# Attention scores as seven block products for each pair of key chunks, half-features and query blocks

## The chip, the cores and the metric

One core of a Trainium2 chip runs the whole program. The time is the device time of one launch in microseconds, as a median over launches. The profile is one execution of its own, with its own time. The engines of the core are TensorE (PE, with its weight loads PEld), VectorE (DVE), ScalarE (ACT), GpSimd (POOL) and SyncE (SP), which issues nearly all DMAs.

## The reference

A block of a transformer: a layer norm, then attention with one head of 512 features, and beside it a mixture of 64 low-rank experts of which each token takes 16; both are added to the input.

```python
xn = _layernorm(x)                                   # x: (2, 2048, 2048)
# attention
qkv = einsum('bsc,cf->bsf', xn, Wqkv) + bqkv         # (2, 2048, 3 * 512)
q, k, v = qkv.reshape(2, 2048, 3, 512) ...
attn = softmax(einsum('bqd,bkd->bqk', q, k) / sqrt(512))
att = einsum('bqd,dc->bqc', einsum('bqk,bkd->bqd', attn, v), Wo) + bo
# experts
scores = einsum('bsr,er->bse', einsum('bsd,rd->bsr', xn, Wq_w), keys)
gate = softmax over the 16 greatest of the 64 scores, 0 elsewhere
z = einsum('bsd,nd->bsn', xn, A_w)                   # 64 experts x 8
ffn = einsum('bsn,on->bso', gate * z, B_w) * 2
return x + att + ffn
```

All is float32.

## The kernel before

**Arithmetic.** Each float32 operand of a large product is split into a high part (a cast to the rounded type `fp32r`, `split_hi`, on ACT, L123) and a low part (the rest, `split_lo`, on DVE, L126). A product of two operands is three matmuls into one PSUM bank, low x high, high x low and high x high (`PASSES`, L60; `product`, L128). A matmul is 128x128 weights against 512 moving columns.

**Stages.** The 4096 tokens are 8 blocks of 512 (`NB`), four to a sequence (`BPB`). First come the projections: q, k, v, the router and the experts' first product; for the last three pairs of blocks these run as seven phases P1, P2, P6, P5, P3, P7, P4 of Strassen's scheme (`phase`, L755), each with steps on DVE and ACT dealt out beside its matmuls by `beside` (L663). Then comes the attention stage (L1226 to L1281). Last comes the output projection, `multiply` at L1164 and its neighbours, also by Strassen's scheme, for both the attention and the experts at once. P1 and P2 of that scheme share a PSUM bank: P2 is added onto P1.

**What the projections leave for the attention.** `feature_out` (L499) takes one 128-feature tile of q or k for a block out of PSUM, adds the bias, splits it into high and low parts and stores both ([128, 2, 512], 512 KB) to `q_d` or `k_d` in DRAM. `values_out` (L274) does the same for v.

**The attention stage.** A step `s` is one query block of 512 (`blk`) and one chunk of 128 keys (`k`, 16 a sequence). `score` (L935) multiplies the chunk's four feature tiles (`kt`, weights) with the block's (`qt`, moving): 4 x 3 matmuls into one bank, the scores transposed, keys on partitions. ACT copies the bank to SBUF (L950), DVE keeps a running maximum (L954, L956). After a block's 16 chunks `maxes` (L958) reduces the maximum over partitions, and `spread` (L982) lays it on all partitions with a matmul. `soft` (L990) subtracts it, takes the exponential on ACT, splits the result into `ph` and adds the sum `L`. `weigh` (L1005) loads the chunk's values `vt` and multiplies: for each of the four feature tiles three matmuls onto that tile's bank, over 16 chunks. At the end of a block the sum goes through two matmuls and a reciprocal (L1024 to L1027), the four banks are scaled (L1032), get their bias (L1033) and go to DRAM.

In program order each step scores chunk `s`, softens chunk `s - 18` and weighs chunk `s - 21` (`LAG`, L32); so scores and weighted values alternate on PE, with 21 steps of scores alone at the front and 21 of weighted values alone at the end. Four of the seven banks of `acc` (L100) hold a block's values, three serve the scores.

Beside it, `combos` (L1051) makes the sums of output weights that the last stage needs: loads, four additions on POOL, two stores, for eight pieces. In the last 12 steps and after, the first splits of the output weights (`moving`, L1063) and of its moving operands (`ahead`, L1211) are made.

**Order.** The scheduler of the language orders each engine's queue by program order as priority, among what its own model finds ready; `with behind(...)` keeps the instructions in its block behind a named one on the same engine. Tiles named by a `Ring` share slots in turn, and a tile waits until the readers of the one before it in the slot are done. Each engine runs its queue in order.

Of the kernel before, what the change touches and what calls it, by code (L numbers as in the profile page):

```python
# [16 lines left out]
P = 128  # L17
C = 2048
NCH = C // P
D = 512  # L20
# [11 lines left out]
LAG = 21  # L32
# [31 lines left out]
def attn_ffn_kernel(ctx: ExitStack, tc, x, xT, wq, wv, wob, bqk, bv, bo, keysT, out):  # L64
# [6 lines left out]
    KC = 2 * ND  # L71
# [66 lines left out]
    q_d = [scratch(f"q_d{i}_", ND) for i in range(NB)]  # L138
    k_d = [scratch(f"k_d{i}_", ND) for i in range(NB)]
# [359 lines left out]
    def feature_out(i, f, ps, gx, u=None):  # L499
        kind, n = divmod(f, ND)  # L500
        if kind < 2:
            ev = r_ev([P, 2, T], FR, "ev")
            b = bqk_sb[:, f : f + 1]
            if u is None:
                nc.scalar.activation(ev[:, 0, :], ps, AF.Identity, bias=b)
                nc.vector.scalar_tensor_tensor(
                    ev[:, 1, :], ps, b, raw(ev[:, 0, :]), ALU.add, ALU.subtract
                )
            else:
                v = raw(ev[:, 1, :])  # L510
                nc.vector.scalar_tensor_tensor(v, ps, b, u, ALU.add, ALU.add)
                split_hi(ev[:, 0, :], v)
                split_lo(ev[:, 1, :], v, ev[:, 0, :])
            store((k_d if kind else q_d)[i][n], raw(ev))
# [148 lines left out]
    def beside(j, ph):  # L663
# [18 lines left out]
        if ph == "P6":  # L682
            return [], mixed(
                sum_steps(j, nc.vector, b10, b10, b00, ALU.subtract),
                sum_steps(j, nc.vector, b00, b11, b00, ALU.subtract), split_steps(j, "P5", *b00),
                s0[:-2] if more else [],
            )
        if ph == "P5":
            steps = mixed(split_steps(j, "P3", *b11), s1[:-2] if more else [])
            return [], s0[-2:-1] + steps[:6] + s0[-1:] + steps[6:] if more else steps  # L690
        if ph == "P3":
            n = x_steps(j + 1, *b00) if more else ([], [])
            steps = mixed(split_steps(j, "P7", *b01), n[1][:2])
            return n[0], s1[-2:-1] + steps[:3] + s1[-1:] + steps[3:] if more else steps
        if ph == "P7":
            n = x_steps(j + 1, *b10) if more else ([], [])
            return n[0], mixed(split_steps(j, "P4", *b10), n[1][:2])
# [4 lines left out]
        return [], []  # L702
# [106 lines left out]
    NSTEP = NB * NK  # L809
    kt, qt, S, pt_, M, L, av, rl_ = {}, {}, {}, {}, {}, {}, {}, {}  # L810

    def load_k(b, kb):
        for dc in range(ND):
            t = r_kt([P, 2, T], FR, "kt")
            nc.sync.dma_start(raw(t), k_d[b * BPB + kb][dc])
            kt[b, kb, dc] = t

    def load_q(blk):
        for dc in range(ND):
            t = r_qt([P, 2, T], FR, "qt")  # L820
            nc.sync.dma_start(raw(t), q_d[blk][dc])
            qt[blk, dc] = t
# [68 lines left out]
    for j in PAIRS:  # L891
        for ph in PHASES:
            if j == PAIRS[-1] and ph == "P7":
                sA, sB, sC, sD = GROUPS
                r_kt = big(*sC, *sB, *T_SLOTS[:8])
                r_qt = big(*sD, 6, 7, 8, 9)
            if j == PAIRS[-1] and ph == "P4":
                load_q(0)
                load_k(0, 0)
                load_k(0, 1)  # L900
# [3 lines left out]
    s_slots = [*sA, *T_SLOTS[8:], 27, 28]  # L904
    r_sp = big(*s_slots)
# [3 lines left out]
    r_mbc = half(4)  # L909
    r_L = half(5, 6)  # L910
# [3 lines left out]
    r_tw = Ring(sb, "B25", "B26", "B29", "G8", "G9")  # L914
    r_ph = wide(0, 1, 2, 3)
    r_vt = wide(4, 5, 6, 7)
# [18 lines left out]
    def score(s):  # L935
        blk, k = divmod(s, NK)
        b = blk // BPB
        ps = acc()
        sl = slice((k % NT) * P, (k % NT + 1) * P)
        for dc in range(ND):  # L940
            product(
                ps, lambda a: kt[b, k // NT, dc][:, a, sl], lambda c: qt[blk, dc][:, c, :],
                dc == 0, dc == ND - 1,
            )
# [412 lines left out]
```

## Time and profile before

| | us |
|---|---|
| median of 3 runs | 2640.55 |
| lowest and highest | 2639.7, 2644.24 |
| the profiled execution's own time | 2641.34 |
| its span, first to last instruction | 2639.6 |
| first score matmul to last weighted value | 1320 to 2026 |

In the profile a group of instructions is a line of the code with its engine, operation, output and inputs; "busy" is the time in which at least one of them ran, "mean" the duration of one, and instructions of one engine overlap in part. "Idle before" is what the engine stood still ahead of them, with what released it. A row of stages gives busy time of each engine, the granted TensorE clock, the mean busy share of the 16 DMA engines and what they moved.

### The profile page before, as it was taken

The numbers are of one execution on the slowest core, as the hardware profiler recorded it, in microseconds if no ns is written. First come the engines' busy times: TensorE is split into PE (matmuls) and PEld (weight loads), VectorE is DVE, ScalarE is ACT, GpSimd is POOL, SyncE is SP. The second block draws the span as 40 slices with busy tenths as digits, with TensorE's granted clock in tenths as the row PEclk, the third lists the DMA queues.
The fourth block names the chain that finished last, engine by engine and source line by source line (L and its number), as shares of the span: only waits on it lengthen the run. The fifth ranks groups of instructions, "written<-read, shape, count | busy, mean of one in ns | idle before, by whom it ended". The sixth has DMA issues, their size and how long they took to land.

```text
span 2639.6 us, 33827 instructions
## 1 busy us (share of the span) xinstructions
PE 2624.7 (99%) x12881; PEld 2220.4 (84%) x12881; DVE 1822.3 (69%) x2495; ACT 863.6 (33%) x1285; POOL 571.8 (22%) x347
## 2 busy tenths in 40 slices
PE   8999999999999999999999999999999999999999
PEld 7889888888888888888888888888888888888887
DVE  7667859867878688756545675456568776797775
ACT  4333323333333333333233343334344222232221
POOL 1312420000000000000101111000012656566664
PEclk9999999999999999999999999999999999999999
DMA  6777884768556683546725476634468545565543
GB/s 234 254 260 256 310 299 166 228 222 295 162 173 221 218 291 129 176 128 222 287 97 192 143 268 227 210 112 144 130 204 267 172 162 165 177 222 172 180 158 106
DMA packets 243395, 530.42 MB, mean 201 GB/s; under 512 B 21608, under 2 KB 87200, under 8 KB 243232
## 3 DMA queue, kind: packets, MB, share of 16 engines
q1 hardware_dynamic: 230272, 498.37, 55.9%
q10 hardware_dynamic: 12960, 29.89, 3.4%
q8 instruction: 101, 1.65, 0.2%
q14 instruction: 62, 0.51, 0.1%
HBM read 393.80 MB, written 134.38 MB: 200 GB/s over the span
## 4 chain that ended last, share of the span: by engine, by line
PE 98%; DVE 1%; DMA 0%; ACT 0%; issue 0%; SPq 0%; ACTq 0%; DVEq 0%
PE acc L131 75%; PE acc L1172 23%; DMA xs<-in_x 0%; DVE st L196 0%; PE acc L366 0%; DVE xh L126 0%; PE misc L451 0%; PE misc L984 0%; DVE wh L126 0%; DMA v_d<-vs 0%; PE misc L1024 0%; PE misc L1025 0%; PE misc L481 0%; ACT xh L123 0%; ACT xs L357 0%
## 5 line engine op out<-in xcount | busy, mean ns | idle before, releaser
L131 PE MATMUL acc<-t,pw 128*128 128x512 f32 x3024 | 693.4, 390 | 0.0
L131 PEld LDWEIGHTS acc<-t,pw 128*128 128x128 f32 x3024 | 565.4, 188 | 117.4
L1172 PE MATMUL acc<-wb,s 128*128 128x512 f32 x2688 | 609.4, 389 | 0.0
L1172 PEld LDWEIGHTS acc<-wb,s 128*128 128x128 f32 x2688 | 504.5, 188 | 104.8
L131 PE MATMUL acc<-ph,vt 128*128 128x512 f32 x1536 | 367.5, 390 | 0.0
L131 PE MATMUL acc<-qt,kt 128*128 128x512 f32 x1536 | 366.0, 389 | 0.0
L131 PEld LDWEIGHTS acc<-ph,vt 128*128 128x128 f32 x1536 | 287.4, 188 | 62.1 <-DVE ot L1032 1.2
L131 PEld LDWEIGHTS acc<-qt,kt 128*128 128x128 f32 x1536 | 288.1, 188 | 60.3 <-issue 0.2
L1156 POOL TENSOR_TENSOR xo<-xo,bo_bc 128x512 f32<-128x512 f32 x128 | 217.0, 1702 | 551.0 <-DMA xo<-in_x 292.1
L123 ACT CAST pw<-pw 128x1024 fp32r<-128x1024 f32 (+1 forms) x168 | 177.7, 1058 | 373.8 <-PE acc L131 252.3
L126 DVE TENSOR_TENSOR pw<-pw 128x1024 fp32r<-128x1024 f32 (+1 forms) x168 | 217.6, 1296 | 67.3 <-ACT pw L123 67.1
L131 PE MATMUL acc<-xh,wh 128*128 128x512 f32 x1152 | 263.6, 390 | 0.0
L131 PEld LDWEIGHTS acc<-xh,wh 128*128 128x128 f32 x1152 | 215.6, 188 | 45.0
L131 PEld LDWEIGHTS acc<-pw,t 128*128 128x128 f32 x2016 | 245.8, 188 | 3.2 <-DVE yv L746 2.0
L131 PE MATMUL acc<-pw,t 128*128 128x264 f32 x2016 | 246.5, 283 | 1.8 <-DVE yv L746 1.8
L123 ACT CAST s<-xz 128x1024 fp32r<-128x1024 f32 x112 | 118.0, 1055 | 371.5 <-PE acc L1172 301.5
L126 DVE TENSOR_TENSOR s<-xz,s 128x1024 fp32r<-128x1024 f32 x112 | 173.2, 1548 | 42.0 <-ACT s L123 42.0
L126 DVE TENSOR_TENSOR ph<-sp,ph 128x512 fp32r<-128x512 f32 x128 | 93.0, 729 | 120.6 <-ACT ph L123 119.8
L956 DVE TENSOR_TENSOR M<-M,sp 128x512 f32<-128x512 f32 x112 | 79.1, 706 | 124.3 <-ACT sp L950 123.8
L521 POOL TENSOR_TENSOR zt<-zt,g 128x512 f32<-128x512 f32 x24 | 37.5, 1572 | 496.4 <-DVE zt L520 148.1
L126 DVE TENSOR_TENSOR wh<-wu,wh 128x512 fp32r<-128x512 f32 x96 | 99.3, 1055 | 58.8 <-ACT wh L123 58.8
L950 ACT COPY sp<-acc 128x512 f32<-128x512 f32 x128 | 74.9, 586 | 182.6 <-PE acc L131 182.5
(149 smaller groups left out, 2365.9 us busy)
## 6 DMA issues: line engine op xcount, KB each, us to landing
vt<-v_d SPq DMA_DIRECT2D x128, 512.0 KB, 3.5
pw<-sq_d SPq DMA_DIRECT2D x72, 512.0 KB, 3.6
xz<-oz_d SPq DMA_DIRECT2D x64, 512.0 KB, 4.9
xo<-in_x SPq DMA_DIRECT2D x128, 256.0 KB, 3.5
out_y<-xo SPq DMA_DIRECT2D x128, 256.0 KB, 2.3
pw<-in_wq SPq DMA_DIRECT2D x54, 512.0 KB, 4.0
wu<-in_wq SPq DMA_DIRECT2D x48, 512.0 KB, 5.8
xq<-in_xT SPq DMA_DIRECT2D x48, 512.0 KB, 6.8
```

Of the source, the lines that this page charges most:

```text
L123: return nc.scalar.copy(hi, src)
L126: return (eng or nc.vector).tensor_tensor(lo, src, raw(hi), ALU.subtract)
L131: last["pe"] = nc.tensor.matmul(ps, st(a_), mv(b_), start=first and n == 0, stop=end and n == 2)
L521: nc.gpsimd.tensor_tensor(zt, zt, gx[n], ALU.mult)
L950: nc.scalar.copy(st, ps)
L956: nc.vector.tensor_tensor(M[blk], M[blk], st, ALU.max)
L1156: nc.gpsimd.tensor_tensor(xs, xs, bo_bc[q // (NB // 2 * NH), c], ALU.add)
L1172: nc.tensor.matmul(ps, st[a_][:, kk, sl], mv[b_], start=not more and kk == 0 and n == 0, stop=kk == ND - 1 and n == 2, skip_group_check=more,)
```

## The change

Keys, features and queries are each cut in two: two chunks of 128 keys, two halves of 256 features, two blocks of 512 queries. The four score tiles of a chunk pair and a block pair took 4 x 12 = 48 matmuls; they become seven products of 256 features, 7 x 6 = 42 matmuls. `ORDER` names them as the other stages do.

- `feature_out` stores q and k unsplit, 256 KB a tile.
- `key_steps` loads a block's keys for one 128-feature tile of each half, makes the seven key operands with four subtractions or additions of 256 elements, splits them, and writes them to `kp_d`. The steps for key blocks 0 to 4 run beside the last pair's phases P6, P5 and P4, those for 5 to 7 inside the attention stage.
- `query_steps` makes the four sums of queries of a block pair and writes them to `qs_d`; pairs 0 and 1 beside phases P3 and P7, pairs 2 and 3 in the attention stage. `query_load` and `query_split` fetch and split an operand.
- `key_load` streams the key operands through a ring of five tiles of two operands each, for every block pair anew.
- `score(g)` makes one product and combines it; a block pair's 56 products come in a row, and weighted values of the pair before are dealt between them. So the first 65 products run without weighted values and the last pair's values without scores.
- `soft` subtracts and takes exponentials two chunks at a time; `ph` has three slots in place of four.
- `combos` adds on DVE in place of POOL and has eight DMAs of 256 KB in place of four of 512 KB.

```diff
 def feature_out(i, f, ps, gx, u=None):
-            ev = r_ev([P, 2, T], FR, "ev")
+            ev = r_ev([P, T], F32, "ev")
             if u is None:
-                nc.scalar.activation(ev[:, 0, :], ps, AF.Identity, bias=b)
-                nc.vector.scalar_tensor_tensor(
-                    ev[:, 1, :], ps, b, raw(ev[:, 0, :]), ALU.add, ALU.subtract
-                )
+                nc.scalar.activation(ev, ps, AF.Identity, bias=b)
             else:
-                v = raw(ev[:, 1, :])
-                nc.vector.scalar_tensor_tensor(v, ps, b, u, ALU.add, ALU.add)
-                split_hi(ev[:, 0, :], v)
-                split_lo(ev[:, 1, :], v, ev[:, 0, :])
-            store((k_d if kind else q_d)[i][n], raw(ev))
+                nc.vector.scalar_tensor_tensor(ev, ps, b, u, ALU.add, ALU.add)
+            store((k_d if kind else q_d)[i][n // 2][:, n % 2, :], ev)
...
+    ORDER = ("P1", "P6", "P2", "P5", "P3", "P7", "P4")
+    ks = {"R": big(25, 26), "st": big(27, 28, 29, 9)}
+    def key_steps(kb, d):
...
+        def one(step):
+            a00, a01, a10, a11 = (quad(a, h) for a in range(2) for h in range(2))
+            tt = nc.vector.tensor_tensor
+            out()
+            src = {"P1": a00, "P2": a01, "P4": a11, "P5": a11, "P7": a10, "P6": a00, "P3": a01}[step]
+            if step == "P5":
+                tt(a11, a10, a11, ALU.add)
...
+            st = ks["st"]([P, 2, 2, P], FR, "kst")
+            split_hi(st[:, :, 0, :], src)
+            split_lo(st[:, :, 1, :], src, st[:, :, 0, :])
+            v["out"] = kp_d[kb][ORDER.index(step)][:, :, :, d, :], raw(st)
...
+    def query_load(j, n):
...
+        hi, lo = (r_qt([P, 2, T], FR, "qt") for k in range(2))
+        nc.sync.dma_start(raw(lo), src)
+        qop[j, n] = hi, lo
...
+    def key_load(i):
...
+        t = r_kt([P, 2, 2, 2, P], FR, "kt")
+        for o in range(2):
+            st, n = divmod(2 * i + o, 7)
+            j, m = divmod(st, NKS)
+            kb = j // 2 * BPB + m // 2
+            last["sp"] = nc.sync.dma_start(raw(t[:, o]), kp_d[kb][n][:, m % 2])
+            kop[2 * i + o] = t[:, o]
...
+                r_qt = big(*sC, *sD, *sA, *sB)
+                r_kt = big(*T_SLOTS[:3], 25, 26)
...
-    r_ph = wide(0, 1, 2, 3)
-    r_vt = wide(4, 5, 6, 7)
+    r_ph = wide(0, 1, 2)
+    r_vt = wide(3, 4, 5, 9)
...
+    def score(g):
+        st, n = divmod(g, 7)
+        j, m = divmod(st, NKS)
+        b0, b1 = 2 * j, 2 * j + 1
+        step = ORDER[n]
+        more = step == "P2"
+        ps = bank["P1"] if more else acc()
+        bank[step] = ps
+        k, q = kop.pop(g), qop[j, n]
+        for d in range(2):
+            for i, (a, c) in enumerate(PASSES):
+                last["pe"] = nc.tensor.matmul(
+                    ps, k[:, a, d, :], q[c][:, d, :],
+                    start=not more and d == 0 and i == 0, stop=d == 1 and i == 2,
+                    skip_group_check=more,
+                )
+        tt = nc.vector.tensor_tensor
+        if step == "P1":
+            nc.scalar.copy(unit(b0, m)[:, 1, :], ps)
+        u, v = S[b0, m], S.get((b1, m))
+        if step == "P6":
+            tt(u[:, 1, :], u[:, 1, :], ps, ALU.add)
+        elif step == "P2":
+            nc.scalar.copy(u[:, 0, :], ps)
+        elif step == "P5":
+            tt(unit(b1, m)[:, 1, :], u[:, 1, :], ps, ALU.add)
+            greatest(b0, m, 0)
+        elif step == "P3":
+            tt(v[:, 0, :], v[:, 1, :], ps, ALU.add)
+            greatest(b1, m, 0)
+        elif step == "P7":
+            tt(v[:, 1, :], v[:, 1, :], ps, ALU.add)
+            tt(u[:, 1, :], u[:, 1, :], ps, ALU.add)
+            greatest(b1, m, 1)
+        elif step == "P4":
+            tt(u[:, 1, :], u[:, 1, :], ps, ALU.add)
+            greatest(b0, m, 1)
...
+        if k % 2 == 0:
+            nc.vector.tensor_tensor(
+                u, u, mbc[blk].unsqueeze(1).to_broadcast([P, 2, T]), ALU.subtract
+            )
+            nc.scalar.activation(u, u, AF.Exp, scale=SCALE)
...
+    begin = [NG1 * (j + 1) + (9 if j in (0, NPAIR - 1) else 5) for j in range(NPAIR)]
+    for i in range(4):
+        key_load(i)
...
+    for n, (kb, d) in enumerate(((5, 0), (5, 1), (6, 0), (6, 1))):
+        deal(2 + 11 * n, key_steps(kb, d))
...
+    deal(NG1 + 10, [small_ring] + key_steps(7, 0) + key_steps(7, 1))
+    deal(NG1 + 38, query_steps(2, r_tp), 2)
+    deal(2 * NG1 + 7, query_steps(3, r_tp), 2)
...
+    for j in range(1, NPAIR):
+        deal(NG1 * j - 14, [lambda j=j: query_load(j, 0), lambda j=j: query_split(j, 0)], 4)
+        for n in range(1, 7):
+            deal(NG1 * j - 7 + n, [lambda j=j, n=n: query_load(j, n), lambda j=j, n=n: query_split(j, n)], 3)
...
+    for g in range(begin[-1]):
+        if g < total:
+            score(g)
+            if g % 2:
+                key_load(g // 2 + 4)
...
+        for i in range(NPAIR - 1):
+            if begin[i] <= g < begin[i + 1]:
+                to = NW * i + NW * (g + 1 - begin[i]) // (begin[i + 1] - begin[i])
+                while done < to:
+                    weigh(done)
+                    done += 1
```

Here `NG1` is 56 (products of a block pair), `NW` 128 (weighted products of a block pair, three matmuls each), `NKS` 8 (chunk pairs) and `NPAIR` 4.

## The prediction

> **What bounds the kernel now.** I read the page from the top: first the busy shares and the chain that ended last, then the matmul groups, then the chain in order of time inside the attention stage, then the busy time of every engine by stage.
>
> ```profile
> PE 2624.7 (99%) x12881; PEld 2220.4 (84%) x12881; DVE 1822.3 (69%) x2495; ACT 863.6 (33%) x1285; POOL 571.8 (22%) x347
> ...
> PE 98%; DVE 1%; DMA 0%; ACT 0%; issue 0%; SPq 0%; ACTq 0%; DVEq 0%
> ...
> L131 PE MATMUL acc<-ph,vt 128*128 128x512 f32 x1536 | 367.5, 390 | 0.0
> L131 PE MATMUL acc<-qt,kt 128*128 128x512 f32 x1536 | 366.0, 389 | 0.0
> ```
>
> TensorE is the bound: 98% of the chain is PE. The scores are 1536 matmuls (`qt,kt`), the weighted values another 1536 (`ph,vt`); no idle time stands before either. That a busy PE really issues without gaps is seen in the chain in order of time:
>
> ```profile
> 1369.71 76.36 PE acc L131 x336
> 1446.07 0.43 PE misc L984
> 1446.50 13.80 PE acc L131 x60
> 1460.30 0.24 PE misc L1024
> 1460.54 0.23 PE misc L1025
> 1460.77 73.59 PE acc L131 x324
> ```
>
> 336 matmuls in 76.36 us and 324 in 73.59 are 227.2 ns each (the 389 of the groups is latency, not pace). So a matmul taken out is worth 0.2272 us as long as nothing else becomes late.
>
> **The gain.** Before, 8 blocks x 16 key chunks x 12 matmuls = 1536. After, 4 block pairs x 8 chunk pairs x 7 products x 6 matmuls = 1344. 192 x 0.2272 = 43.6 us, all in a stage where PE never waits. Everything else is what that gain may lose; no term below can be negative, since PE has no wait left to give up in these stages. The new stage needs 1344 + 1536 matmuls = 654 us, plus 8 x (0.43 + 0.24 + 0.23) = 7, so 661 us.
>
> **VectorE.** What it has to do follows from these rows:
>
> ```profile
> 1388.11 1.89 DVE L993 TENSOR_TENSOR sp<-sp,mbc 128x512 f32<-128x512 f32 x3
> ...
> 1391.51 2.88 PE L131 MATMUL acc<-ph,vt 128*128 128x512 f32 x12
> 1391.71 0.59 ACT L950 COPY sp<-acc 128x512 f32<-128x512 f32 x1 [0.69 <-PE acc L131]
> ```
>
> Three operations of 512 take 1.89 us where one takes 0.68, so back to back each costs 0.605. In the same way 1024 elements cost about 1.14 (1.22 alone, less 0.08) and 256 about 0.345 (0.41 to 0.43 for 248 and 264 elements alone, less 0.075). Per chunk pair and block pair the scheme needs 6 PSUM additions and 4 maxima: 10 x 0.605 = 6.05, times 32 = 191 after the saved first maxima. The exponentials need 16 subtractions of 1024, 32 low parts and 30 sums per pair: 18.2 + 19.4 + 18.2 = 55.8, times 4 = 223. Each block's end (maximum spread 3.0, reciprocal 3.35, four outputs 2.4, low part 0.6) is 9.4, times 8 = 75. New in the stage: 21 query low parts x 1.14 = 24; 6 key steps x 11 operations x 0.345 = 23; query sums 16 x 0.605 = 10; `combos`, moved from POOL, 32 x 0.605 = 19; the weight splits and sums for the output projection, there before too, 16. Total 581 of 661 us, 88%; before it was 55% to 63%. By stretch: 85 of 88.6 in the scores of the first pair alone (65 products x 1.363 before the first weighted value), 403 of 470 in the middle, 93 of 102 after the last score.
>
> ```profile
> 1099.00:1143.00 44.00, 44.00 (x241) 38.41 (x240) 29.03 (x31) 13.28 (x14) 3.53 (x2) 1.00 0.42 136
> 1143.00:1188.00 45.00, 45.00 (x251) 39.50 (x250) 21.36 (x24) 13.32 (x14) 0.00 (x0) 1.00 0.45 142
> 1228.00:1231.00 3.00, 3.00 (x15) 2.47 (x14) 2.52 (x3) 2.39 (x3) 0.00 (x0) 1.00 0.72 170
> 1320.00:1378.00 58.00, 58.00 (x257) 47.64 (x256) 24.06 (x45) 17.64 (x33) 0.00 (x0) 1.00 0.29 103
> 1730.00:1818.00 88.00, 88.00 (x388) 72.39 (x387) 48.67 (x78) 31.79 (x54) 0.00 (x0) 1.00 0.41 132
> 1969.00:2026.00 57.00, 57.00 (x250) 46.42 (x249) 51.62 (x73) 27.74 (x44) 15.56 (x5) 1.00 0.81 275
> 2026.00:2100.00 74.00, 74.00 (x328) 61.29 (x327) 53.69 (x53) 20.32 (x23) 37.47 (x23) 1.00 0.60 199
> ```
>
> Columns: stretch, length, busy PE, weight load, DVE, ACT, POOL, clock, DMA share, GB/s. The row of 1969 shows DVE 51.6 of 57 us (91%) with PE full: so 86% in the middle and 91% in the tail need not cost PE anything; 96% in the first stretch is beyond what was seen. I take **0 for the tail** (bounds 0 and 5) and **1 for the middle** (0 and 8). Moving `combos` to DVE is free: with POOL adding beside it, the subtraction L993 takes 853 ns mean against 685 without, and windows with it hold some 55 us of DVE instead of 48.7 for two `combos`, more than the 4.8 us they cost on DVE itself; they issue 8 DMAs each in place of 4, at times when SP has some 2.9 us per product. ACT keeps room: it stays near 32 us a block, of 88 before and 82 after.
>
> **DMA.** The last two columns give a full-share rate: 103/0.29 = 355 GB/s for 4 KB rows, 199/0.60 = 332 for 2 KB rows, 170/0.72 = 236 around the four `gd<-gT` writes in 512 B pieces, which is how the key operands are written. In the first score stretch must move: 65 key operands of 0.262 MB (17.0 MB, 51 us), 8 key loads (2.1 MB, 6), 28 key writes in 512 B pieces (7.3 MB, 31), 7 query operands and 3 value tiles (5.2 MB, 15). That is 103; less 6 for the eight operands fetched earlier, 97 of 88.6 us: 8.6 late. All at 355 would give 87 and no delay. With DVE operations at their full 0.68 (95.5 us) another 7 is lost. SP has 111 DMAs to issue there at 0.32 to 0.57 us, 36 to 63 of 88.6. Behind a late transfer, or a key write that waits for DVE, stand the next ones in SP's queue, key operands too, only 8 products ahead. At the stretch's end the second pair's query operands can be fetched only when the first pair's last product of the same kind is done: 7 products or 9.5 us ahead, where landing (7.4 median of `qt`), cast (1.05) and low part (1.14) take 9.6; there the delay should show first. Bounds 0 and 16; **I take 8**, the nearest rows' value. The Trainium skill ("DMA: Bandwidth & Descriptors", Specifications) puts full rate at 512 B and above; by that the 31 would be 21, this term nothing, and the time 2605; the 236 measured here differs, and I keep it.
>
> Ahead of the stage, phases P6 and P5 of the last pair get 3 and 5 key steps, each 1.6 us of loads and 7.8 of writes. P6: 0.42 x 44 + 28 = 47 of 44; P5: 0.45 x 45, less four `qt` loads that go (5.9), + 47 = 61 of 45. So 19 us of transfers spill into P3. PE is hurt only if weights come late; SP issues them between the key writes, at most four of which (4.4 us) can be under way in the four-slot ring. Weight loads land in 3.6 us, up to 10.7, with no PE wait now. **I take 3**; bounds 0 and 19. VectorE there rises to 21.4 + 19 = 40 of 45, covered as above. The plain stores of q and k save 48 low parts and half the bytes; in a stage bound by PE that is worth nothing.
>
> **Buffers.** P2 adds into P1's bank, so PE waits for ACT's copy of P1 while P6 (1.36 us) runs. The copy begins 0.20 after the next product and takes 0.59: 0.57 to spare, less when a 1.05 us cast is ahead on ACT; behind that wait stand all later matmuls. **I take 1** (0 to 5; in the middle 2.3 weighted products more lie between). At a block's end four banks wait for reciprocal and outputs, with one score fewer in between than now; the trace has 1.2 us of such waits over eight blocks, four outputs each time would be 2 x 8. **I take 3** (1 to 16). The change from the projections to the scores: key operands can be fetched during P4, since their slots are free after P7. **0** (to 7, if they stood behind the last value stores).
>
> **Sum.** -43.6 + 8 + 3 + 1 + 3 + 1 = -27.6. The profiled execution took 2641.3 us (span 2639.6); that becomes 2613.7. The median of the runs is 0.8 lower, so **2613 us**. All lower bounds together lose 1: 2598. All upper ones lose 76: 2673.
>
> The skill ("TensorE: Matmul & The Clock Gate", Part 1) says PE falls to half clock after an idle window of about 3.4 us. The clock is 1.00 in each row above, as no PE wait here is that long after the start; if the 8 us came in one piece, the recovery would add an estimated 1.7 us.
>
> **Rivals.**
> *Nothing is late.* The buffers take up all peaks, as PE without a gap at 91% DVE suggests: 2598 to 2604. Against it: the 97 of 88.6 us of DMA.
> *The transfers set the pace* wherever key operands are written: the whole 16 and 19 lost, 2626 to 2635. For it: 512 B pieces at 236 GB/s. Against: weights have slack of several us.
> *Slower: VectorE paces the scores.* Each product needs its bank freed by an addition queued in order on DVE, with four of seven banks held by the values. If additions stand behind waiting softmax work so that an operation costs on average 25% more than 0.605, the stretches need 106, 504 and 116 of 88.6, 470 and 102 us: 66 lost, **2663 us**. It decides from about 21% on (0.735 us an operation). For it: DVE idles 120 us before `ph` for ACT and 124 before `M`, a sign of its in-order waits. Against: those waits harm nobody now, at 91% in the tail too.
>
> **Chances.** 2604 to 2626, my forecast: 0.35. Nothing late: 0.25. Transfers pace: 0.12. Within 0.2% (about what a measurement of this kernel can tell from no change, 5.3 us): 0.05. Slower: 0.23, most of it between 2646 and 2670. So faster 0.72, same 0.05, slower 0.23. The range is 2598 to 2652, with some 0.15 above it and 0.03 below; faster cases alone end at 2635.
>
> **What would show it.** Score matmuls x1344 at 227 ns; DVE near 88% in the stage; PE waits, if I am right, in the first 89 us of scores and the two phases P6 and P5, with a key tile's DMA or a DVE addition as releaser; DMA share near 1 there. If the attention stage is 661 us and free of waits, the DMA term is wrong; if PE waits for DVE all through the middle, the rival on VectorE is right.

## The result and the profile after

The changed kernel took 2653.95 us (median of 6 runs, 2648.07 to 2655.96) against 2642.05 of the kernel before on the same chip (6 runs, 2639.70 to 2644.24): a ratio of 1.0042, 95% interval 1.0029 to 1.0055. It is slower by 0.4%, where 1.1% faster was forecast; the side that was given 0.23 came true, and the time lies 2 us above the stated range. The profiled execution took 2654.26 us, its span is 2652.4.

The page first: busy shares, chain, and the two matmul groups of the attention.

```profile
PE 2604.3 (98%) x12689; PEld 2197.6 (83%) x12689; DVE 1982.9 (75%) x2827; ACT 858.9 (32%) x1249; POOL 519.9 (20%) x315
...
PE 31%; DVE 1%; DMA 0%; issue 0%; ACT 0%; SPq 0%; DVEq 0%; ACTq 0%
...
L129 PE MATMUL acc<-ph,vt 128*128 128x512 f32 x1536 | 381.0, 393 | 6.1 <-DMA vt<-v_d 2.8
...
L1062 PE MATMUL acc<-qt,kt 128*128 128x512 f32 x1344 | 342.1, 397 | 16.9 <-ACT sp L1069 10.3
```

The 192 matmuls are gone. The chain's shares add up to some 32% only: followed back from the last instruction, it breaks off near 1770 us, so it can't be set beside the 98% of before and tells nothing of the stage's first part. What does tell is the idle time before both groups (16.9 and 6.1 us), where there was none. PE's waits from the phases P6 and P5 to the first score, and then in the attention stage, tell for what (us in total, times, longest):

```profile
PE acc L129 <- ACT t L121: 4.6, 1, 4.6
PE acc L129 <- DVE yv L755: 2.3, 1, 2.3
```

```profile
PE acc L1062 <- ACT sp L1069: 10.3, 3, 5.9
PE misc L1115 <- DVE mq L1105: 4.7, 4, 1.8
PE acc L1062 <- DVE qt L124: 4.4, 5, 1.3
PE acc L129 <- DMA vt<-v_d: 2.8, 1, 2.8
PE acc L129 <- DVE ph L124: 1.9, 1, 1.9
PE acc L1062 <- DMA kt<-kp_d: 1.9, 1, 1.9
```

The greatest one is ACT's copy of P1 (L1069), for which P2 waits because it adds onto the same bank. Only 1.9 us of these waits are for a key operand's transfer. All waits in the stage, smaller ones too, come to 27.5 us.

To see how much was lost where, I cut the time at four points of PE's timeline (first score, first weighted value, last score, first matmul of the output projection) and took off what the matmuls of each piece need at 0.2272 us: 398 in the scores alone (90.4 us), 2030 in the middle (461.2, with 6 for the small matmuls of the block ends 467), 451 in the tail (103.2 with its share of those). "Ahead" is how much later than before (1320.15) the scores begin. The same cut of every kernel profiled, in us lost:

| kernel | ahead | scores alone | middle | tail | sum | time of that execution |
|---|---|---|---|---|---|---|
| predicted | 3 | 8 + 1 | 3 + 1 | 0 | 16 | 2613.7 |
| changed kernel | 12.7 | 27.2 | 7.4 | 11.0 | 58 | 2654.26 |
| a_no_keys56 | 17.5 | 10.6 | 4.9 | 10.9 | 44 | 2639.74 |
| c_loads_early | 17.0 | 16.2 | 4.5 | 7.4 | 45 | 2640.95 |
| d_half_stream | 12.7 | 14.8 | 10.3 | 10.0 | 48 | 2644.47 |
| e_phases_ahead | 13.3 | 16.4 | 7.4 | 6.9 | 44 | 2639.98 |
| f_maxima_later | 15.3 | 25.7 | 6.7 | 10.3 | 58 | 2653.9 |
| g_tail_loads_ahead | 16.2 | 25.9 | 7.2 | 3.6 | 53 | 2649.62 |
| h_all_ahead | 9.3 | 15.5 | 6.7 | 3.8 | 35 | 2632.3 |
| j_keys67_later | 10.7 | 17.0 | 17.6 | 5.7 | 51 | 2647.41 |
| i_keys4_later | 14.1 | 8.5 | 13.8 | 4.5 | 41 | 2638.14 |

Sum less 43.6, less some 1 us that the stage of before loses by the same cut, is the change of the span: 58 - 45 = 13 here, and 2652.4 - 2639.6 is 12.8. Four rows (changed kernel, a, f, g) have the same code up to the first score and differ there by 12.7 to 17.5, so a difference of 5 us in that column is no finding by itself. In the first score stretch the changed kernel and g still have the same code, f all but its last ten products, and they lose 25.7 to 27.2. The rows of c_loads_early and h_all_ahead are the fastest run of each kernel, and so favourable ones.

What a wait in the first score stretch looks like, from the timeline of all engines (start, duration, engine, line, operation; in brackets the idle time before it and what ended it):

```profile
1338.22 11.70 PE L1062 MATMUL acc<-qt,kt 128*128 128x512 f32 x42 [2.47 <-ACT sp L1069]
...
1346.42 0.43 DVE L288 TENSOR_TENSOR vs<-acc,xv 128x264 f32<-128x264 f32 x1 [7.53 <-DMA v_d<-vs]
...
1351.46 1.12 SPq L834 DMA_DIRECT2D kr<-k_d  x2
...
1354.90 0.40 ACT L121 CAST kst<-kr 128x256 fp32r<-128x256 f32 x1 [6.75 <-DMA kr<-k_d]
1355.21 0.58 ACT L1069 COPY sp<-acc 128x512 f32<-128x512 f32 x1
```

ACT stands for 6.75 us before a cast of raw keys (`kr`) whose load SP issued only at 1351.46; P1's copy is the next instruction in ACT's queue and has to stand with it; PE gets going at 1355.84, after 5.92 us. Eight us earlier DVE stood for 7.53 us in the same way, before the last projection's values, whose slot was still being stored. Here neither ACT nor DVE was short of time. Each had one instruction at the head of its queue that waited for a transfer. SP was one more link between the two: it issued nothing from 1342.52 to 1348.00, as the next store of those values waited for DVE, and the load of `kr` stood behind that store. From SP's waits in the stretch:

```profile
SPq L162 <- DVE vs L124: 5.4, 1, 5.4
```

The stretch as a whole, its first 30 us, what lies between, its last 22 us, and a window of the middle stage (start and end, length, busy PE, weight load, DVE, ACT, POOL, granted clock, DMA share, GB/s):

```profile
1332.85:1450.45 117.60, 100.86 (x401) 77.97 (x399) 88.95 (x169) 33.05 (x65) 0.00 (x0) 0.93 0.92 304
1332.85:1362.85 30.00, 21.60 (x80) 16.65 (x79) 15.88 (x35) 6.87 (x17) 0.00 (x0) 0.83 0.88 273
1362.85:1428.45 65.60, 61.83 (x255) 49.49 (x254) 51.68 (x97) 16.53 (x35) 0.00 (x0) 0.95 0.96 313
1428.45:1450.45 22.00, 17.44 (x68) 11.83 (x66) 21.40 (x39) 9.65 (x13) 0.00 (x0) 1.00 0.85 321
...
1824.00:1846.00 22.00, 22.00 (x98) 18.22 (x98) 22.00 (x34) 9.28 (x12) 0.00 (x0) 1.00 0.90 309
```

By the matmuls that start in each piece, 12 us are lost in the first, 8 in the second and 7 in the third. DVE is busy for 89 us of the 117.6 (76%); at 1824 it is busy all the time and PE loses nothing, so a busy DVE alone doesn't make PE wait. But in the last 22 us it is busy for 21.4 (97%), and there PE's five waits for the low parts of the next query operands (`qt`, 4.4 us) end with DVE. The DMA share of the stretch is 92% at 304 GB/s, which is 35.8 MB.

### The profile page after: what moved, and what is told of

It reads as the page before. It is cut to its first block, busy times and chain, and to the rows that moved or that the text cites. A ratio compares the mean times of both kernels' runs of the same rounds, so it can differ in the third digit from the quotient of the medians.

```text
span 2652.4 us, 34800 instructions
## 1 busy us (share of the span) xinstructions
PE 2604.3 (98%) x12689; PEld 2197.6 (83%) x12689; DVE 1982.9 (75%) x2827; ACT 858.9 (32%) x1249; POOL 519.9 (20%) x315
## 5 line engine op out<-in xcount | busy, mean ns | idle before, releaser
L1320 POOL TENSOR_TENSOR xo<-xo,bo_bc 128x512 f32<-128x512 f32 x128 | 210.8, 1654 | 914.5 <-DMA bo_bc<-in_bo 609.6
L129 PE MATMUL acc<-ph,vt 128*128 128x512 f32 x1536 | 381.0, 393 | 6.1 <-DMA vt<-v_d 2.8
L1062 PE MATMUL acc<-qt,kt 128*128 128x512 f32 x1344 | 342.1, 397 | 16.9 <-ACT sp L1069 10.3
L1062 PEld LDWEIGHTS acc<-qt,kt 128*128 128x128 f32 x1344 | 256.1, 192 | 77.0 <-ACT sp L1069 11.8
L124 DVE TENSOR_TENSOR wh<-wu,wh 128x512 fp32r<-128x512 f32 x96 | 81.0, 860 | 99.4 <-ACT wh L121 99.4
L121 ACT CAST ph<-sp 128x512 fp32r<-128x512 f32 x128 | 78.9, 619 | 167.2 <-PE acc L129 161.1
L1325 DVE TENSOR_TENSOR xo<-xo,acc 128x512 f32<-128x512 f32 x128 | 86.9, 680 | 54.8 <-PE acc L1336 26.0
L121 ACT CAST t<-xq 128x1024 fp32r<-128x1024 f32 x84 | 88.0, 1051 | 94.3 <-DVE xq L648 41.0
```

Of the source, the lines that this page charges most:

```text
L121: return nc.scalar.copy(hi, src)
L124: return (eng or nc.vector).tensor_tensor(lo, src, raw(hi), ALU.subtract)
L129: last["pe"] = nc.tensor.matmul(ps, st(a_), mv(b_), start=first and n == 0, stop=end and n == 2)
L1062: last["pe"] = nc.tensor.matmul(ps, k[:, a, d, :], q[c][:, d, :], start=not more and d == 0 and i == 0, stop=d == 1 and i == 2, skip_group ...
L1320: nc.gpsimd.tensor_tensor(xs, xs, bo_bc[q // (NB // 2 * NH), c], ALU.add)
L1325: nc.vector.tensor_tensor(xs, xs, ps, op)
```

## The experiments

The theory after the result: ACT and DVE stand behind key steps that wait for their own transfers, and what PE needs stands behind them. The rivals: VectorE and ScalarE have too much to do; or the transfers of the stretch as a whole set its length.

**a_no_keys56: no key preparation in the first score stretch.** Key blocks 5 and 6 are not prepared; the scores of the second sequence take the operands of blocks 1 and 2 instead, so the stream is the same.

```diff
             kb = j // 2 * BPB + m // 2
+            kb = {5: 1, 6: 2}.get(kb, kb)
...
-    for n, (kb, d) in enumerate(((5, 0), (5, 1), (6, 0), (6, 1))):
-        deal(2 + 11 * n, key_steps(kb, d))
```

> The key steps of key blocks 5 and 6, dealt inside the first stretch of scores, are left out, and their operands are read from blocks 1 and 2 (so pairs 2 and 3 score other keys). The stretch took 117.6 us for 399 matmuls that need 90.6. Theory one, in-order engines stand behind key casts and low parts that wait for their own transfers: without them the stretch is 92 to 97 us, with at most the query waits at its end left (some 5 us), and the program 20 to 25 us shorter, near 2630. Theory two, the key stream that PE reads sets the pace: the stream is still there, so the stretch stays above 105 us. Theory three, VectorE is full there: it loses 15 us of its 85, and the waits for query low parts (4.4 us) shrink but the long waits for ACT's copy of P1 stay: above 105 us.

The stretch fell from 117.6 to 101.0 us, and one run took 2639.74. That is less than the other two theories gave (above 105) and more than mine did (92 to 97); the time is 10 us above mine. So 16.6 of the 27 lost there come with the four key steps, by their work, their waits or their transfers: the stretch moved 262 GB/s x 101 us = 26.5 MB. One wait of 3.4 us for P1's copy stayed at the stretch's start, where the key steps of phase P4 are still being finished.

**b_keys_pool: the arithmetic of all key steps on GpSimd**, so that ACT and DVE have nothing of it in their queues.

```diff
-            tt = nc.vector.tensor_tensor
+            tt = nc.gpsimd.tensor_tensor
...
-            split_hi(st[:, :, 0, :], src)
-            split_lo(st[:, :, 1, :], src, st[:, :, 0, :])
+            nc.gpsimd.tensor_copy(st[:, :, 0, :], src)
+            split_lo(st[:, :, 1, :], src, st[:, :, 0, :], nc.gpsimd)
```

> All arithmetic of the key steps (casts, sums, low parts, 18 operations each, all 16 steps) goes to POOL; transfers are the same. Theory one (in-order ACT and DVE stand behind key work that waits for transfers): the waits move to POOL, where nothing else is late, so the first stretch falls from 117.6 to 92 to 100 us and the phases before the scores from 12.6 us late to under 4: 2615 to 2625 in all, faster than before. Theory two (transfers set the pace): within 5 us of the changed kernel, 2649 to 2659. Theory three (VectorE is full): VectorE gains 15 us in the stretch, but POOL's reads slow it; 2640 to 2650.

Far off: 2716.6 us (2713.68 to 2724.99), ratio 1.0286 (1.0266 to 1.0306). The scores begin at 1380.95, 61 us later than before; the stretch takes 129.5. PE's waits ahead of the first score:

```profile
PE misc L454 <- ACT qT L449: 11.3, 1, 11.3
PE acc L129 <- ACT t L121: 10.0, 1, 10.0
PE acc L129 <- ACT pw L121: 9.8, 2, 8.0
PE acc L129 <- DVE pw L124: 8.9, 3, 6.7
```

On average a low part takes 856 ns on POOL against 420 on DVE, a sum 972 to 1077 against 416 to 490, and the phases now wait for operands of their own (`t`, `pw`) on ACT and DVE. Which transfers or slots pass the lateness on was not followed further; the run doesn't tell the theories apart.

**c_loads_early: the same work and transfers, but the raw keys are loaded a step ahead** (two steps' loads beside the first key operands, four slots instead of two), in the first stretch alone.

```diff
-    ks = {"R": mid(0, 1), "st": wide(0, 1, 2, 3, 4, 5)}
+    ks = {"R": mid(2, 3, 0, 1), "st": wide(0, 1, 2, 3, 4, 5)}
...
+    for n, steps in enumerate(early):
+        if n > 1:
+            deal(2 + 11 * (n - 1), steps[:1])
+        deal(3 + 11 * n, steps[1:])
```

> In the first stretch the loads of the key steps of blocks 5 and 6 are issued one step (some 15 us) earlier, into four slots in place of two; all else stays. Theory one in its narrow form (ACT waits at the head for the key load, 5.9 us once): the wait of ACT's casts for the key loads goes, the stretch falls by 8 to 14 us to 104 to 110, the program to 2640 to 2646. If it is the store slots or the transfers at large: no change beyond 3 us.

In the profiled execution, the fastest of ten, the stretch took 106.6 us, 11 less with nothing taken out of it: that much was waiting, not work. The time is 2646.68 (2640.95 to 2652.51, 10 runs), ratio 1.0017 (1.0006 to 1.0027), just above the 2640 to 2646 expected; the median is 7 us below the changed kernel's. ACT's greatest wait before a key cast changed its cause. In the changed kernel, from the first score to the first weighted value:

```profile
ACT kst L121 <- DMA kr<-k_d: 20.2, 7, 7.4
```

and here:

```profile
ACT kst L121 <- DMA kp_d<-kst: 24.3, 14, 5.3
```

The load is there in time, and the cast now waits for its output slot, which is still being stored. PE still waits 5.1 us for P1's copy behind it. The stretch, and the part between its first 30 and its last 22 us, and these last, in the columns of above:

```profile
1337.10:1443.70 106.60, 96.77 (x401) 76.00 (x399) 88.75 (x168) 32.20 (x63) 0.00 (x0) 0.97 0.99 337
1367.10:1421.70 54.60, 54.60 (x243) 45.22 (x242) 48.74 (x91) 15.21 (x31) 0.00 (x0) 1.00 1.05 366
1421.70:1443.70 22.00, 17.26 (x65) 11.13 (x63) 21.65 (x40) 9.32 (x13) 0.00 (x0) 1.00 0.88 320
```

It moves as much as before, 337 GB/s x 106.6 us = 35.9 MB, at a DMA share of 0.99. Yet the transfers are not what holds PE: in the 54.6 us between, at a share of 1.05 (a packet counts where it starts), PE never stands. What is still lost lies at the two ends: 8 us in the first 30, around one wait of 4.2 us for P1's copy, and 8 in the last 22, where DVE is busy for 21.65.

**d_half_stream: half the traffic of key operands**, all key steps in place. Only the first operand of each tile is loaded and stands for both.

```diff
-            last["sp"] = nc.sync.dma_start(raw(t[:, o]), kp_d[kb][n][:, m % 2])
-            kop[2 * i + o] = t[:, o]
+            if o == 0:
+                last["sp"] = nc.sync.dma_start(raw(t[:, o]), kp_d[kb][n][:, m % 2])
+            kop[2 * i + o] = t[:, 0]
```

> Every second key operand is not loaded; its product uses the one before it in the tile (other scores). This takes 29 of the 59 MB of the key stream away and leaves all engine work. Theory two (transfers set the pace): the first stretch falls below 98 us, the tail keeps its 114, the program 20 us shorter. Theory one (engines in order behind key casts that wait for their own loads and stores): these come sooner with less traffic, but wait still: 105 to 114 us. Theory three (VectorE): unchanged, 115 to 118.

The stretch took 105.2 us, one run 2644.47:

```profile
1332.80:1438.00 105.20, 94.99 (x399) 75.53 (x397) 86.22 (x166) 33.37 (x65) 0.00 (x0) 0.97 0.80 251
```

26.4 MB at a share of 0.80: the transfers have room, and the stretch is hardly shorter than c's, as expected if waits set it (105 to 114). PE waits 6.8 us for P1's copies, and ACT 14.6 in place of 20.2 before a cast for its load. Less traffic shortens the waits as earlier loads do, and leaves the same two ends: 9 us are lost in the first 30 and 5 in the last 22.

The second round took the four places one by one.

**e_phases_ahead: raw keys one step ahead in the phases P6, P5 and P4**, with four slots, and other slots for stores in P4.

```diff
+    KSL = [key_steps(m // 2, m % 2) for m in range(10)]
+    def key_part(a, b):
+        return [
+            st for m in range(a, b)
+            for st in (KSL[m + 1][:1] if m < 9 else []) + KSL[m][1:]
+        ]
...
-    ks = {"R": big(25, 26), "st": big(27, 28, 29, 9)}
+    ks = {"R": Ring(sb, "B25", "B26", "H6", "H7"), "st": big(27, 28, 29, 9)}
```

> Only the key steps ahead of the scores change: each step's loads are issued one step (about 9 us) earlier, into four slots in place of two, and P4's two steps store from four slots in place of two. Same instructions, same bytes. In the changed kernel the scores begin 12.6 us later than before (1332.8 against 1320.2) and lose 10.7 us more in their first 20 us. If ACT and DVE stand at the head of their queues for key loads and store slots: the scores begin at 1321 to 1326 and the first 20 us lose under 6. If it is the number of bytes in P6 and P5 or DVE's load there: they begin at 1330 to 1335 as now.

Where it was expected to help it did not: the scores begin at 1333.4, 0.6 us later than in the changed kernel. The wait for `t` fell from 4.6 to 1.0, the one for `yv` rose from 2.3 to 4.9. But the stretch behind it took 106.8 instead of 117.6: phase P4 no longer hands its unfinished key steps on to the scores. One run took 2639.98.

**f_maxima_later: the block's maxima three products later, its two spreads one and four** in program order, as their matmul waits for DVE.

```diff
-            if n == 1:
+            if n == 4:
                 maxes(2 * j - 2)
-            if n in (0, 2):
+            if n in (1, 6):
...
-                    spread(2 * j - 1 - n // 2)
+                    spread(2 * j - 1 - n // 6)
```

> The partition maxima of a pair's first block go three products later and both spreading matmuls one and four products later in program order. In the changed kernel PE waits 4.7 us in four places for the spread's operand from DVE, with some more lost to the clock. If DVE is late only at the change of pairs, these waits fall below 1.5 us, the middle from 474.4 to 468 to 471 us. If DVE is late throughout, other waits for DVE take their place and the middle stays within 2 us.

Nothing was gained: 2653.9. The waits for `mq` fell from 4.7 to 3.0 us, a new one of 2.0 for the scaled outputs `ot` came in their place, and the middle is 6.7 against 7.4. That is what was expected if DVE is late throughout the middle and not only where pairs change.

**g_tail_loads_ahead: output weights loaded one piece at a time in the tail, and split two chunks later**, instead of two pieces loaded and split at once with value tiles behind them in SP's queue.

```diff
-        if d == 0 and c in (2, 6, 10, 14):
-            for kk in range(0, ND, 2):
-                with behind("sp"):
-                    for st in moving(0, STEPS[c // 4], kk):
-                        st()
+        if d == 0 and c % 2 == 0 and 2 <= c <= 18:
+            with behind("sp"):
+                if c > 2:
+                    splits[c // 2 - 2]()
+                if c < 18:
+                    one_load, one_split = moving(0, STEPS[(c - 2) // 4], (c - 2) % 4)
+                    one_load()
+                    splits.append(one_split)
```

> After the last score the loads of the output weights go one by one, two chunks ahead of their splits, in place of two at once just before them. In the changed kernel the tail takes 114.2 us for 102.3 us of matmuls; PE waited 2.8 us for values queued on SP behind a load of output weights that waited for its slot, and 1.9 us for a low part behind splits and a reciprocal on DVE. If it is SP's queue: the tail falls to 106 to 109 us. If it is DVE's load (some 91%): it stays at 112 to 116.

The tail fell from 114.2 to 106.8 us. The waits of 2.8 us for `vt` and 1.9 for `ph` are gone from it. DVE's work there is the same, so the 11 us of the tail were mostly SP's order.

**h_all_ahead: e, f and g together, and the early loads of c** with other slots.

```diff
+    early = [key_steps(kb, d) for kb, d in ((5, 0), (5, 1), (6, 0), (6, 1))]
     for i in range(4):
         key_load(i)
+        if i < 2:
+            early[i][0]()
```

> The three edits of this call and early loads of the key steps in the first stretch together. If the lateness is that of in-order queues behind transfers, the parts add: 12.6 to about 4 ahead of the scores, 27 to about 14 in the first stretch, 9 to 5 in the middle, 12 to 6 in the tail: some 30 us off the changed kernel's 2653, so 2618 to 2630, faster than before by 0.5 to 0.9%. If the transfers or DVE as a whole were the bound, lateness only moves to the next place: 2643 to 2653.

2638.85 us (2632.3 to 2646.74, 12 runs) against 2642.77 (17 runs): ratio 0.9985 (0.9976 to 0.9995). That is faster than before by 0.15%, and less than expected (2618 to 2630). What is left at the start of the scores:

```profile
PE acc L1070 <- ACT sp L1077: 5.5, 1, 5.5
```

It is the first P1 copy. ACT stands 5.29 us before the last key casts of phase P4, whose loads were issued at 1328.47.

The third round asked for the place of the key steps, and for the price of a wait by itself.

**j_keys67_later: h, with key block 6 prepared in the next pair of query blocks**, where block 7 is prepared already.

```diff
-    early = [key_steps(kb, d) for kb, d in ((5, 0), (5, 1), (6, 0), (6, 1))]
+    early = [key_steps(kb, d) for kb, d in ((5, 0), (5, 1))]
...
-    deal(NG1 + 10, [small_ring] + key_steps(7, 0) + key_steps(7, 1))
+    later = [key_steps(kb, d) for kb, d in ((6, 0), (6, 1), (7, 0), (7, 1))]
+    deal(NG1 + 10, [small_ring] + later[0] + later[1] + later[2])
+    deal(NG1 + 56, later[3])
```

> h_all_ahead with the preparation of key block 6 moved out of the first score stretch into the next pair of query blocks, where block 7's stands (a product and its share of weighing take 3 us there, against 1.6); the same work and the same transfers in all. Theory (in-order waits behind key preparation make the stretch late): the stretch falls from 105.9 to 97 to 102, the middle grows by 0 to 3, the time is 2630 to 2637. Rival (the lateness is VectorE's and the queue's total, and goes with the work): the middle grows by what the stretch loses, and the time stays 2636 to 2642.

My theory missed: 2645.68 us (2638.74 to 2649.6, 10 runs), ratio 1.0005 (0.9995 to 1.0014). The stretch took 107.4 and the middle lost 17.6 instead of 6.7. Half the key steps in the stretch gave nothing, though it moved only 282 GB/s x 107.4 us = 30.3 MB at a share of 0.85. Between the ends there was nothing left to gain, for PE doesn't stand there in h either; 11 us are lost in the first 30, behind one wait, and 7 in the last 22 (from the timeline):

```profile
1335.89 0.40 ACT L121 CAST kst<-kr 128x256 fp32r<-128x256 f32 x1 [6.51 <-DMA kr<-k_d]
...
1341.96 8.20 PE L1070 MATMUL acc<-qt,kt 128*128 128x512 f32 x25 [8.27 <-ACT sp L1077]
```

**i_keys4_later: j, with key block 4 taken out of phase P4** and prepared in the first stretch, beside block 5.

```diff
-            [lambda n=n: query_ready(0, n) for n in range(7)], key_part(8, 10)
+            [lambda n=n: query_ready(0, n) for n in range(7)], []
...
-    early = [key_steps(kb, d) for kb, d in ((5, 0), (5, 1))]
+    early = [key_steps(kb, d) for kb, d in ((4, 0), (4, 1), (5, 0), (5, 1))]
```

> j_keys67_later with the preparation of key block 4 also moved, out of the last projection phase into the first score stretch, which then prepares blocks 4 and 5. Theory (the wait of 5.5 us at the first P1 copy stands behind that preparation): it is gone, the stretch is 98 to 103 with the same work in it as in h_all_ahead, less that wait, and the time is 2628 to 2636. Rival (the wait is the query operands' own chain): a wait of 3 us or more stays within the first 12 products, the stretch is 104 or more, and the time 2637 to 2643.

The long wait for P1's copy is gone (1.2 us is left of 8.3), and the stretch takes 98.9 us with as many key steps in it as h has. The time is 2636.6 us (2629.3 to 2639.16, 6 runs) against 2643.93 (15 runs), ratio 0.9969 (0.9957 to 0.9980): faster than before by 0.3%, a little above the range expected. The middle gives part of it back (13.8 lost). Whether this one beats h is not shown: their intervals, 0.9957 to 0.9980 and 0.9976 to 0.9995, overlap. Its stretch, the part between its first 30 and its last 22 us, and these last, in the columns of above:

```profile
1334.28:1433.13 98.85, 91.98 (x399) 73.86 (x398) 84.22 (x155) 30.76 (x58) 0.00 (x0) 1.00 0.97 326
1364.28:1411.13 46.85, 46.85 (x209) 38.78 (x208) 40.02 (x72) 12.54 (x26) 0.00 (x0) 1.00 1.01 336
1411.13:1433.13 22.00, 16.32 (x66) 11.53 (x65) 21.38 (x40) 9.60 (x13) 0.00 (x0) 1.00 0.92 336
```

326 GB/s x 98.85 us is 32.2 MB, 3.7 less than in c: ten key operands were on their way before the first score where c had four, and two writes left over from phase P4 are gone. Of the 8.5 us still lost, 7 lie in the last 22 us, where DVE is busy for 21.4 and PE waits 3.3 us for the first `ph` and 2.3 for query operands; between, at a DMA share of 1.01, none is. So the first end is cured, and the second one is not. No run took work off DVE there, so whether it is DVE's load or the order of its queue stays open.

**k_before_waits: the kernel before, with three waits put into its first score stretch.** A matmul by a tile of zeros (nothing is added to the scores) needs a tile that POOL makes by additions after the copy of the product before.

```diff
+    LATE, zero_of = {4: 1, 10: 3, 16: 3}, {}
...
+            if dc == 1 and s in LATE:
+                nc.tensor.matmul(
+                    ps, zero_of.pop(s), qt[blk, dc][:, 0, :], start=False, stop=False
+                )
...
+        for n in range(LATE.get(s + 1, 0)):
+            nc.gpsimd.tensor_tensor(slow, st if n == 0 else slow, st, ALU.add)
```

> The kernel before with three waits of TensorE put into its first score stretch, where it has none: a matmul by a tile of zeros, which GpSimd makes by one, three and three additions of 128x512 after the copy of the product before (1.7 us each in other rows, so waits of about 2, 5.5 and 5.5 us, 13 in all). Nothing else is late there. Theory (each wait is followed by matmuls at a lower granted clock): the stretch of 60.5 us grows by the waits and by 2 to 2.5 us more behind each, about 20 us in all, and the time is 2658 to 2664. Rival (a wait costs its own length, and the slow matmuls of the changed kernel come from something else, such as traffic): matmuls right behind each wait take 227 ns, the stretch grows by 13, the time is 2653 to 2657.

POOL's additions took 1.27 to 1.50 us on average, not 1.7, so the waits were shorter than meant: 7.2 us in all. PE's timeline:

```profile
1336.19 0.50 PE L945 MATMUL acc<-qt,zero 128*128 128x512 f32 x1 [1.19 <-POOL zero L963]
1336.52 17.43 PE L131 MATMUL acc<-qt,kt 128*128 128x512 f32 x76
1356.91 0.79 PE L945 MATMUL acc<-qt,zero 128*128 128x512 f32 x1 [2.96 <-POOL zero L963]
1357.50 17.83 PE L131 MATMUL acc<-qt,kt 128*128 128x512 f32 x72
1378.38 0.80 PE L945 MATMUL acc<-qt,zero 128*128 128x512 f32 x1 [3.04 <-POOL zero L963]
```

and PE by window (start and end, length, busy PE, granted clock, DMA share, GB/s):

```profile
1341.00:1354.00 13.00, 12.95 (x58) 1.00 0.00 0
1354.00:1357.00 3.00, 0.09 (x1) 0.97 0.00 0
1357.00:1361.00 4.00, 4.00 (x11) 0.59 0.02 4
1361.00:1365.00 4.00, 4.00 (x20) 1.00 0.00 0
```

The stretch grew from 60.5 to 73.5 us, by 13.0 for 7.2 us of waits. 0.7 is the three added matmuls; the other 5.1 are matmuls at a lower clock, nearly all of it behind the two longer waits. Behind the wait of 2.96 us the granted clock was 0.59 for 4 us, with the DMA share at 0.02: 11 matmuls where the next window of the same length holds 20. Behind the wait of 1.19 us, 76 matmuls took 17.43 us, which is full pace. The time was 2656.1 us (2651.47 to 2658.35, 4 runs), ratio 1.0045 (1.0030 to 1.0060), 12 us for 7.2 of waits. It falls into the rival's range of times only because the waits were shorter; that matmuls run at 227 ns right behind every wait is refuted.

## Why the prediction was wrong

- **The gain** was as worked out: 192 matmuls fewer, and 1344 + 1536 at 0.2272 us wherever PE is neither waiting nor just behind a wait.
- **VectorE's load** was right: 85 us worked out for the first stretch, 84 to 89 measured. The rival that VectorE paces the scores (2663 us) comes near the measured time and is not what happened in most of the stretch: DVE is idle a quarter of it, and where it is full (the window at 1824) PE doesn't wait. Two things of its argument hold. Additions stand behind waiting work in order; and in the last 22 us, at 97%, PE's waits of 4.4 us end with DVE. The prediction named that place, where the second pair's query operands are due, but with landing, cast and low part in a row and no full queue on DVE before the low part.
- **The first score stretch** is the step that failed: 8 for late transfers and 1 for P1's copy, 27.2 measured. The term took the pace of the transfers for what makes PE late. The runs show otherwise: where the DMA engines are at their limit and nothing else stands in the way, PE loses nothing (54.6 us in c, 46.9 in i). The loss of the changed kernel is 12 us in the first 30, 8 in the next 66 and 7 in the last 22. The first two come, but for one wait of 1.9 us for a key operand's transfer, from what was in no term: each key step puts a cast and up to two VectorE operations at the head of in-order queues before its load or its output slot is there. I saw this only as "1 (0 to 5)", where a cast of 1.05 us stands ahead of P1's copy, not a cast that itself waits 6.75 us for a load; PE's waits for that copy are 10.3 us, and a lower clock comes behind them. c shows 11 of it (the same work and bytes, only earlier loads); i, with P4's key steps out of the way, brings the first 12 down to 1.
- **The sum of that term** had errors both ways, too. 35.8 MB were moved, not 31.6, and the eight operands fetched earlier should not have come off, as eight are fetched ahead at the end as well (all at 355 GB/s, with them off, is 83 us and not 87). The rates were too low: 304/0.92, 337/0.99 and 326/0.97 (changed kernel, c, i) are 330 to 340 GB/s at full share, where 31.6 MB in 103 us are 307; so the 236 for the key writes, read off 3 us, was low.
- **Ahead of the stage** I took 3 (0 to 19) and 12.7 came, inside the bounds. I had named weights that come late; PE waited for `t` (4.6 us), whose cast on ACT waited for DVE's `xq`, and for `yv`, which is DVE's own. Both kinds of lateness show there (DVE before a key step, all engines up to the end of the wait for `t`, DVE before `yv`):

```profile
1142.58 0.42 DVE L124 TENSOR_TENSOR kst<-kr,kst 128x256 fp32r<-128x256 f32 x1 [3.18 <-ACT kst L121]
1144.00:1152.80 8.80, 4.26 (x20) 3.20 (x18) 8.73 (x17) 5.90 (x9) 0.00 (x0) 0.88 0.96 282
1196.41 0.43 DVE L124 TENSOR_TENSOR kst<-kr,kst 128x256 fp32r<-128x256 f32 x1 [2.27 <-ACT kst L121]
```

  DVE first stood for 3.18 us behind a key step, and then was busy for 8.73 of 8.80 us; before `yv` it stood again. Loading raw keys earlier (e) moved the wait from one to the other and gained nothing, so work and waits are not told apart here.
- **The tail** was costed at 0 because a DVE at 91% had been seen beside a full PE. The 11 us there were mostly SP's queue: value tiles behind the output weights' loads; g took 7.4 of them away without touching DVE.
- **Block ends and middle**, 3 + 1: 7.4 measured, with 3.9 us of waits for the maxima's `mq`. f did not move them; what holds them was not found.
- **The clock.** I gave 1.7 us for one recovery, and that size is right, but it comes many times. In the stage the granted clock is one half for 27.3 us, in seven stretches of 3.41 or 6.83 us, such as this one (PE alone, granted clock, DMA share, GB/s):

```profile
1389.68:1393.09 3.41, 3.41 (x10) 0.50 1.01 288
```

  PE stands for 3.7 us of them, and the other 23.6 cost half their length, 12 us. With the 27.5 of waits that is 39 of the 45 lost in the stage; the rest is spread thin. k shows the price without any other lateness: 5.1 us, nearly all behind the two waits of 3 us. The Trainium skill ("TensorE: Matmul & The Clock Gate", Part 1) gives the idle window that halves the clock as about 3.4 us; here 2.96 us was enough, and 1.19 was not. In the changed kernel four waits of 1.8 to 1.9 us were enough, too. But length alone doesn't decide: behind a wait of 2.65 us in k's projections (at 566.26 us) the clock stayed at 1.00.

So 16 us of lateness became 58: 18 more than forecast were lost in the first stretch, 10 ahead of it, 11 in the tail and 3 in the middle. Of what was lost in the stage, a quarter (12 of 45) is the clock.

Open: which of the waits in P6 and P5 could be taken away; what the last 22 us of the stretch need; why the middle loses 7 to 10 us more when block 6 is prepared there, with a ring of two slots (j and i). A version that also spreads those key steps with slots of their own was not tried.

## What to carry to other kernels

When a change adds small operations fed by transfers to an engine that also copies out the accumulators of a TensorE-bound loop, don't sum its busy time: write down what stands behind each of them in its queue, and how long the engine stands if the load or the slot comes a few us late. Issue such loads a whole step ahead, and let no half-finished side work cross into a stage where the accumulators turn over faster. Cut a stretch into pieces before naming its limit: a DMA share of 0.99 over the whole was no limit in the piece where it was highest. Price a TensorE wait of 2 to 3 us at its own length and up to about as much again: here one or two stretches of 3.41 us at half clock came behind most of them, and none behind some.

## What was not expected of the hardware

- A wait of 2.96 us put TensorE at a granted clock of 0.59 over the next 4 us, one of 1.19 us left it at 1.00, with the DMA share at 0.02 beside it. In the changed kernel the mean granted clock of the first stretch is 0.93; in i, whose waits there are 0.9 to 1.4 us but for one of 3.3 at its end, it is 1.00.
- The DMA engines held 99% and 337 GB/s over 107 us of loads mixed with 512 B writes (c), and 97% and 326 GB/s with PE's mean granted clock at 1.00 beside them (i).
- The runs of the changed kernels spread more than those of before: 2632.3 to 2646.74 for h in 12 runs, 2640.02 to 2648.42 for the kernel before in 17 runs on the same chip. That waits which hang on how transfers fall vary from one execution to the next is the likely reason; no run tested it.
